# Sixteen scatters into token lists and the zeros behind them, regrouped on one queue of a fused graph-attention and mixture-of-experts kernel

## The chip, the cores and the metric

The kernel runs on one core of a Trainium2 chip. The time is that of the device, in microseconds, from one execution. An engine here is one of the core's instruction streams: PE multiplies matrices, DVE and ACT compute elementwise, POOL and SP in this kernel mostly issue DMAs.

## What is computed

One layer: graph attention over 4096 nodes with 256 features, then a feed-forward layer of eight experts, of which each row uses its two best. Cut to what matters:

```
# attention, 4 heads of 64
h   = einsum('nd,hdk->hnk', layernorm(x), W)
e   = leaky_relu(s_row[:, :, None] + s_col[:, None, :], 0.2)
att = softmax(where(adj > 0, e, -9e15))
y   = elu(att @ h) + layernorm(x) @ Wr + br
x   = x + gamma * normalised(y) + beta
# experts, 8, hidden width 1024, two for each row
xf  = layernorm(x)
top_w, top_i = top_k(xf @ Wg + bg, 2);  top_w = softmax(top_w)
for e in range(8):
    out += w_dense[:, e] * (gelu(xf @ W1[e] + b1[e]) @ W2[e] + b2[e])
x   = x + out
```

## The kernel before, in words

**Two halves.** The first is the attention. The 4096 rows are taken in four passes of 1024, and PE multiplies without a pause while DVE makes the weights. After a pass its rows are finished, normalised and routed (`route_rows`, from L1243): each row gets its two experts, its two weights, and its two places in the *lists*. The lists are a table in HBM, one stretch per expert; a row of it holds the 256 features, both weights, the row's number and its first expert, 260 numbers (1040 bytes). A row is put there by a scatter, an indirect DMA that POOL issues (L1385): 128 rows in one scatter, two for each 128 rows (first and second expert). A pass of 1024 rows makes 16 scatters; 64 in all.

**The expert tiles.** The second half runs over 27 tiles of one expert each (`todo`, L1989): 9 `early` ones of 256 rows, whose rows come from the first two passes, 8 `mid` ones of 256 rows from the first three, then 8 `final` ones of what is left of each expert, and 2 of `rest`. The early and mid tiles are 0 to 16. For a tile, `fetch` (L1777) has SP load the rows of the list (`load_blocks_of`, L579, a small load `known` and eight of `xr`; the first six tiles are loaded whole by L571 instead), then b2 (L1792), W1 (L600) and W2 (L1799). DVE turns the rows (L1857), `up` (L1864) makes 16 matmuls with W1 into PSUM (L1873; 32 records in the trace) and ACT applies GELU to each of the 8 results (L1877), `down` (L1886) makes two products of 128 rows with W2 (L1907), eight matmuls each. DVE weighs each of them into a buffer `o` (L1920; nine buffers, L1919), and POOL adds it to the rows of the result by an indirect DMA with addition, the *sum* (L1932). Two sums of the same rows of the result may not be under way together, so a sum waits until the one before it has landed.

**The last pass inside the tiles.** The 1024 rows of the fourth pass are not finished before the tiles start. Their work is cut into steps and put between the products of the first tiles (`between`, L1975, called twice a tile, after `up` and after `down`). Each half of the pass, 512 rows, ends with eight scatters; the first half after the second call of tile 3, the second after the second call of tile 4. Then the remaining tiles are planned (`plan_rest`, L439).

**The zeros.** Behind the last row of each expert's list, 512 rows of zeros are written (`tail_cleared`, L500, the DMA is L507), so that a tile which reads past the end finds zeros. One is taken off `tails` at the end of each tile.

**What sets the order.** PE's order in the tiles is written out by hand (`order_of`, L543). POOL's order follows from the order in which the program makes the instructions, from dependences, and for the clears from an explicit one: a clear stands behind the last sum made so far (L510 to L514). An early or mid tile's row loads need not wait for scatters or clears made before them (`needs_of`, L557, `declare_no_dep`), for their rows were written long ago. In the other direction nothing is declared: a scatter or a clear waits for the row loads made before it, as both touch the lists. All SP loads and all POOL scatters, sums and clears go through the same queues in this order:

```
2022            between(2 * i + 1)
2023            if tails:
2024                tails.pop(0)()
```

Of the kernel before, what the change touches and what calls it, by code (L numbers as in the profile page):

```python
# [44 lines left out]
def gat_then_moe(  # L45
# [19 lines left out]
    nc = tc.nc  # L65
# [41 lines left out]
    lists = nc.dram_tensor("lists", [E * LIST, RW], F32, kind="Internal").ap()  # L107
# [111 lines left out]
    def forward(apart, stack):  # L219
# [49 lines left out]
        def tables(tag, width):  # L269

            return {
                "expert": moe_tile(f"expert{tag}", [P, width]),
                "mark": moe_tile(f"mark{tag}", [P, width]),
                "own": moe_tile(f"own{tag}", [P, width, E]),
                "place": moe_tile(f"place{tag}", [P, width]),
                "rows": moe_tile(f"rows{tag}", [P, width]),
                "float": moe_tile(f"float{tag}", [P, 2, width]),
                "int": moe_tile(f"int{tag}", [P, 2, width], I32),
                "past": moe_tile(f"past{tag}", [P, width, E]),
                "upto": moe_tile(f"upto{tag}", [P, E]),  # L280
            }
# [61 lines left out]
        early, mid, rest, final, over = tables("e", EARLY), {}, {}, {}, {}  # L343
# [154 lines left out]
        tails = []  # L498

        def tail_cleared(ends, zeros, e):  # L500

            end = nc.values_load(
                ends[0:1, e : e + 1], engines=[mybir.EngineType.Pool],
                min_val=e * LIST, max_val=e * LIST + N,
                skip_runtime_bounds_check_because="a list holds each token at most once",
            )
            clearing.append(nc.gpsimd.dma_start(  # L507
                lists[bass.ds(end, WT), :].rearrange("(p c) d -> p (c d)", p=CH), zeros
            ).ins)
            tc.add_manual_dep(  # L510
                clearing[-1], added[-1].name,
                mybir.DependencyInfo(mybir.DependencyClass.NoSync, mybir.DependencyReason.DATA),
                reason="one list for each tile, behind its sums",
            )  # L514

        clearing, added = [], []

        listed, earlier = [], []

# [21 lines left out]
        ordered, strict = [False], [False]  # L541
# [9 lines left out]
        def entry(t, row, i, top):  # L551
            return nc.values_load(
                t["int"][0:1, row, i : i + 1], engines=[mybir.EngineType.SP],
                min_val=0, max_val=top, skip_runtime_bounds_check_because=why,
            )
# [20 lines left out]
        def rows_of_job(t, i):  # L576
            return FINAL[i] * Q if t is final else TT

        def load_blocks_of(t, i, xb, known, late):  # L579


            first = entry(t, 1, i, E * LIST - WT)
            n = known.shape[1] * CH
            begun = [nc.sync.dma_start(
                known, lists[bass.ds(first, n), D:].rearrange("(c p) d -> p c d", p=CH)
            )]
            rows = lists[bass.ds(first, rows_of_job(t, i)), :]
            for c in range(DC):
                for a in range(P // Q):
                    here = c * P + a * Q  # L590
                    begun.append(nc.sync.dma_start(
                        xb[ts(a, Q), c], rows[:, here : here + Q].rearrange("(k p) d -> p k d", p=Q)
                    ))
            for ins in begun:
                needs_of(ins.ins, late)

        def load_first(t, i, w1):

            e = entry(t, 0, i, E - 1)
            nc.sync.dma_start(w1, W1[bass.ds(e, 1)].rearrange("o (c p) f -> p (o c) f", p=P))  # L600
# [14 lines left out]
        with ExitStack() as layer:  # L615
# [109 lines left out]
            sums = gat.tile([P, DC, NB], F32)  # L725
# [455 lines left out]
            def load_adj(pool, rows, j, n, bufs):  # L1181

                at = pool.tile([P, n, len(rows)], I32, tag="adj", name="adj", bufs=bufs)
                marks["adj"] = nc.sync.dma_start(
                    at,
                    adjT[j * P : (j + n) * P, rows.start : rows.stop].rearrange(
                        "(t p) i -> p t i", p=P
                    ),
                ).ins
                return at  # L1190
# [52 lines left out]
            def route_rows(b, xe):  # L1243
# [100 lines left out]
                at = small.tile([P, 2, n], I32, tag="at", name="at")  # L1344
                nc.vector.tensor_copy(at, pos)
                if b == 0:
# [33 lines left out]
                    yield  # L1380
                    nc.vector.tensor_tensor(others, others, least, OP.max)

                for t in range(n):
                    for k in range(2):
                        ins = nc.gpsimd.indirect_dma_start(  # L1385
                            lists, bass.IndirectOffsetOnAxis(ap=at[:, k, t : t + 1], axis=0),
                            xe[:, t, :], None,
                        ).ins
                        for i in listed:
                            tc.declare_no_dep(ins, i.name, reason="other places of the lists")  # L1390
                        listed.append(ins)

            def finish_blocks(a):

# [80 lines left out]
            def rows_listed():  # L1475
                return fin.tile([P, HB * TB, RW], F32, tag="xe", name="xe", bufs=1)
# [133 lines left out]
            if not apart:  # L1610

                with tc.tile_pool(name="gen", bufs=2) as work:
# [12 lines left out]
                    for b in range(NB):  # L1625
# [4 lines left out]
                        for j in range(NT):  # L1630
                            if j % 2 == 0:
                                at = load_adj(work, mine, j, 2, 2)
# [15 lines left out]
                        for j in range(NT):  # L1648
                            if j % 2 == 0:
                                at = load_adj(work, mine, j, 2, 2)  # L1650
# [126 lines left out]
        def fetch(t, i):  # L1777

            rows = rows_of_job(t, i)
            nch = -(-rows // CH)  # L1780
            chosen = t is early or t is mid
            near = chosen and i + EARLY * (t is mid) < NEAR
            if near:
                xr = full_rows[i]
                known = xr[:, :, D:]
            else:
                xr = work.tile([P, DC, rows // Q, Q], F32, tag="xr", name="xr")
                known = work.tile([CH, nch, RW - D], F32, tag="known", name="known")
                load_blocks_of(t, i, xr, known, chosen)
            e = entry(t, 0, i, E - 1)  # L1790
            b2b = work.tile([CH, D], F32, tag="b2b", name="b2b")
            nc.sync.dma_start(b2b, b2[bass.ds(e, 1)].to_broadcast([CH, D]))  # L1792
            if t is early and i == 0:
                w1 = w10
            else:
                w1 = work.tile([P, DC, F], F32, tag="w1", name="w1")
                load_first(t, i, w1)
            w2 = work.tile([P, FC, D], F32, tag="w2", name="w2")
            nc.sync.dma_start(w2, W2[bass.ds(e, 1)].rearrange("o (c p) d -> p (o c) d", p=P))  # L1799
            job = {"t": t, "i": i, "xr": xr, "known": known, "w1": w1, "w2": w2, "nch": nch, "b2b": b2b}  # L1800
            job["rows"], job["near"] = rows, near
            job["last"] = t is rest and i == SURE - 1

            job["into"] = out[: N - R] if t is early or t is mid else out
            return job
# [163 lines left out]
        xe = rows_listed()  # L1969
# [5 lines left out]
        def between(n):  # L1975
            if n == 0:
                begun.append(turn_sums(ud))
            for half in range(HB):
                if n == 2 * half:
                    begun.append(last_block(  # L1980
                        b0 + half, u[:, half], begun[0][:, :, :, half], given[half],
                        xe[:, ts(half, TB)],
                    ))
                if n >= 2 * half and ordered[0]:
                    if next(begun[1 + half], "end") == "end" and half == HB - 1:
                        ordered[0] = False
                        plan_rest()

        todo = [(early, i) for i in range(EARLY)] + [(mid, i) for i in range(MID)]  # L1989
# [4 lines left out]
        jobs = [fetch(*todo[0])]  # L1994
        given = []

        def load_full(i):
            xr = work.tile([CH, 2, RW], F32, tag="early", name="early", bufs=NEAR - 1)
            load_rows_of(early, i, xr)
            full_rows.append(xr)  # L2000
# [8 lines left out]
        xT = turn(job)  # L2009
        for i in range(len(todo)):  # L2010
            if i + 1 == len(jobs) and i + 1 < len(todo):
                jobs.append(fetch(*todo[i + 1]))
            nxt = jobs[i + 1] if i + 1 < len(todo) else None
            hT = up(job, xT)
            between(2 * i)
            if nxt:
                xT = turn(nxt)
            giving = down(job, hT)
            next(giving)
            if nxt:  # L2020
                next(giving, None)
            between(2 * i + 1)
            if tails:
                tails.pop(0)()
            job = nxt

        def held(k, top):
# [82 lines left out]
```

## Time and profile before

| | us |
|---|---|
| median of three timed runs | 1259.73 (1257.01 to 1262.62) |
| the profiled execution, timed as the others | 1258.36 |
| its span, first to last instruction | 1256.7 |
| first product of the expert tiles (tile 0) | 777 |
| tiles 6 to 16, where rows are loaded by blocks | 871.7 to 1028.4 |
| 16 scatters of the last pass on POOL | 846.5 to 878.8 |
| 8 clears on POOL | 882.6 to 976.9 |

The page gives each engine's busy time first, then the span in 40 slices, one digit a slice (9 is 90% or more), with the clock granted to PE and the busy share of the 16 DMA engines:

```profile
PE   9999999999999999999999999999999999999997
POOL 4000000001002601006110024135222212122222
PEclk9999999999999999999999999999999999999999
DMA  6333533436533646335375423868898897455662
```

A slice is 31.4 us. From slice 24 on (the expert tiles) the DMA engines are at six to nine tenths, before that mostly at three to five. The groups of POOL's DMAs (count, busy time and mean of one in ns, idle time before them and what ended it):

```profile
L1932 POOL DMA_INDIRECT out<-o,ids x66 | 102.3, 1550 | 325.0 <-DMA out<-o,ids 151.0
L1385 POOL DMA_INDIRECT lists<-xe,at x64 | 89.0, 1391 | 268.0 <-issue 184.8
```

An idle time of POOL costs the kernel nothing by itself. `PEld` is the loading of stationary operands, beside the products. The name behind an arrow is what released the instruction after its wait.

### The profile page before, as it was taken

The page shows a single profiled execution, that of the slowest core. Times are in us where ns is not written, and L with a number is a line of the kernel's source. Part 1 is how long each engine was busy: PE and PEld are TensorE (multiplying, and loading weights), DVE is VectorE, ACT ScalarE, POOL GpSimd, SP SyncE. Part 2 cuts the span into 40 slices and gives each one's busy share as a digit, 9 for nine tenths or more (in the row PEclk, how much of TensorE's full clock was granted, in tenths as well). Part 3 has the DMA queues.
Part 4 walks back from the last instruction along what each step waited for, and adds up shares of the span by engine and source line. Part 5 has one row for each costly group of instructions (what it writes and reads, how often), then busy time and mean ns, then how long its engine had stood idle before and what let it go on. Part 6 is the DMA issues. An engine that isn't in the chain of part 4 may idle for free.

```text
span 1256.7 us, 22720 instructions
## 1 busy us (share of the span) xinstructions
PE 1239.8 (99%) x8872; PEld 647.8 (52%) x8872; DVE 845.1 (67%) x1566; ACT 448.2 (36%) x918; POOL 241.3 (19%) x217
## 2 busy tenths in 40 slices
PE   9999999999999999999999999999999999999997
PEld 5444444332232332332325334888888876666686
DVE  7998887879999989999999996845111211111120
ACT  4332322265522375322655232533332332222322
POOL 4000000001002601006110024135222212122222
PEclk9999999999999999999999999999999999999999
DMA  6333533436533646335375423868898897455662
GB/s 215 118 119 110 167 111 102 157 113 139 181 110 107 224 116 201 107 98 157 112 171 191 122 84 103 269 181 230 218 234 213 215 229 144 106 139 106 138 161 36
DMA packets 155541, 190.23 MB, mean 151 GB/s; under 512 B 72312, under 2 KB 125680, under 8 KB 155040
## 3 DMA queue, kind: packets, MB, share of 16 engines
q1 hardware_dynamic: 133392, 145.39, 39.8%
q0 software_dynamic: 20544, 36.74, 13.2%
q10 hardware_dynamic: 1488, 6.55, 1.4%
q8 instruction: 71, 1.16, 0.4%
q14 instruction: 46, 0.38, 0.1%
HBM read 155.77 MB, written 29.74 MB: 148 GB/s over the span
## 4 chain that ended last, share of the span: by engine, by line
PE 93%; DVE 3%; issue 1%; ACT 1%; DMA 1%; another core or an unknown queue 0%; POOLq 0%; SPq 0%; DVEq 0%; ACTq 0%
PE acc L1198 33%; PE po L1907 18%; PE ph L1873 17%; PE den L1207 17%; PE pr L1053 2%; DVE w L1689 2%; PE ph L1101 2%; PE ptx L1253 0%; DMA early<-lists 0%; PE acc L894 0%; PE pt L780 0%; PE ptr L1491 0%; PE po L1946 0%; PE pl L1264 0%; PE po L875 0%
## 5 line engine op out<-in xcount | busy, mean ns | idle before, releaser
L1198 PE MATMUL acc<-w,ha 128*32 128x512 f32 x4096 | 669.9, 593 | 1.3 <-ACT u L1401 0.9
L1689 DVE SCALAR_TENSOR_TENSOR w<-er,eb,am 128x1024 f32<-128x1024 f32 x496 | 606.1, 1275 | 31.1 <-PE den L1207 31.1
L1207 PE MATMUL den<-w,unit 128*2 128x512 f32 x2048 | 466.9, 592 | 0.1
L1198 PEld LDWEIGHTS acc<-w,ha 128*32 128x32 f32 x4096 | 184.5, 110 | 292.8 <-issue 253.9
L1606 ACT ACTIVATE am<-adj 128x1024 bf16<-128x1024 int32 x124 | 130.6, 1054 | 346.5 <-DVE w L1689 211.7
L1873 PE MATMUL ph<-xT,w 128*128 128x256 f32 (+5 forms) x864 | 231.4, 425 | 2.9 <-ACT hT L1877 2.6
L1907 PE MATMUL po<-w,hT 128*128 128x256 f32 (+1 forms) x1040 | 230.2, 380 | 0.0
L1877 ACT ACTIVATE hT<-ph,bias 128x256 f32<-128x256 f32 (+5 forms) x216 | 111.1, 517 | 292.8 <-issue 185.7
L1907 PEld LDWEIGHTS po<-w,hT 128*128 128x128 f32 (+1 forms) x1040 | 196.2, 189 | 31.5 <-issue 3.1
L1873 PEld LDWEIGHTS ph<-xT,w 128*128 128x128 f32 x864 | 163.8, 191 | 63.4 <-issue 38.7
L1920 DVE SCALAR_TENSOR_TENSOR o<-po,share,b2s 128x256 f32<-128x256 f32 (+2 forms) x66 | 31.5, 479 | 230.1 <-PE po L1907 186.4
L1207 PEld LDWEIGHTS den<-w,unit 128*2 128x2 f32 x2048 | 93.5, 85 | 148.2 <-issue 139.8
L1932 POOL DMA_INDIRECT out<-o,ids x66 | 102.3, 1550 | 325.0 <-DMA out<-o,ids 151.0
L1385 POOL DMA_INDIRECT lists<-xe,at x64 | 89.0, 1391 | 268.0 <-issue 184.8
L1857 DVE STREAM_TRANSPOSE xT<-xr 128x512 f32<-128x512 f32 (+5 forms) x21 | 17.9, 851 | 57.1 <-PE ph L1873 31.2
L1053 PE MATMUL pr<-wr,xT 128*128 128x256 f32 x128 | 30.4, 381 | 0.2 <-ACT er L1147 0.2
L1895 ACT ACTIVATE b2s<-b2b,share 128x256 f32<-128x256 f32 x68 | 30.0, 498 | 0.0
L1121 POOL DMA_DIRECT2D residual<-rb x6 | 4.7, 784 | 121.2 <-DVE rb L1068 121.2
L1441 POOL DMA_DIRECT2D xf<-in_x x6 | 8.1, 1351 | 102.2 <-ACT xf L1440 102.2
L1053 PEld LDWEIGHTS pr<-wr,xT 128*128 128x128 f32 x128 | 24.1, 190 | 5.4 <-issue 0.9
L1101 PE MATMUL ph<-wall,xT 128*128 128x264 f32 x96 | 24.6, 399 | 0.0
L207 ACT ACTIVATE m<-y,off 128x256 f32<-128x256 f32 x48 | 23.7, 495 | 1.1 <-DVE off L215 0.6
(394 smaller groups left out, 617.9 us busy)
## 6 DMA issues: line engine op xcount, KB each, us to landing
adj<-in_adj SPq DMA_DIRECT2D x126, 512.0 KB
w<-in_L_ffn_W SPq DMA_DIRECT2D x54, 1024.0 KB
er<-parts ACTq DMA_DIRECT2D x3, 2048.0 KB
lists<-zeros POOLq DMA_DIRECT2D x8, 520.0 KB
residual<-rb POOLq DMA_DIRECT2D x8, 512.0 KB
rb<-residual SPq DMA_DIRECT2D x8, 512.0 KB
out<-y POOLq DMA_DIRECT2D x8, 512.0 KB
xb<-in_x SPq DMA_DIRECT2D x7, 512.0 KB
```

The costliest lines, as they stand in the source:

```text
L1053: order_of(nc.tensor.matmul(pr[:, k, :], turned[b][:, c, ts(t0 + k, P)], wr[:, c, :], start=(c == 0), stop=(c == DC - 1),))
L1101: order_of(nc.tensor.matmul(phs[t - t0], xT[:, c, ts(t, P)], wall[:, c, :], start=(c == 0), stop=(c == DC - 1),))
L1198: queue(nc.tensor.matmul(acc[half][h // 2][here : here + Q, :], ha[:, j, h * K + g * Q : h * K + (g + 1) * Q], w[half][h], start=(j == 0), ...
L1207: queue(nc.tensor.matmul(den[here : here + HB, :], unit[:, j, h, 1 - half : 1 - half + HB], w[half][h], start=(j == 0 and half == 0), stop ...
L1385: ins = nc.gpsimd.indirect_dma_start(lists, bass.IndirectOffsetOnAxis(ap=at[:, k, t : t + 1], axis=0), xe[:, t, :], None,).ins
L1606: nc.scalar.activation(am, at, AF.Relu, scale=2.0)
L1689: marks["w"] = nc.vector.scalar_tensor_tensor(wh[:, these], er[:, these, h], eb[:, j, h : h + 1], mask[:, these], op0=OP.max, op1=OP.min,).ins
L1873: order_of(nc.tensor.matmul(ph, job["w1"][:, c, ts(f, P)], xT[:, c, :], start=(c == 0), stop=(c == DC - 1),))
L1877: job["gelu"] = nc.scalar.activation(hT[:, f, :], ph, AF.Gelu, bias=job["bias"][:, f : f + 1]).ins
L1907: order_of(nc.tensor.matmul(po[:size], hT[:, f, k * CH : k * CH + size], w2[:, f, :], start=(f == 0), stop=(f == FC - 1),))
L1920: given_out.append(nc.vector.scalar_tensor_tensor(o[:size], po[:size], share[:size, k : k + 1], b2s[k][:size], op0=OP.mult, op1=OP.add,).ins)
L1932: added.append(add().ins)
```

## The change

The eight scatters of each half of the last pass are no longer issued where the half ends. They are kept as functions in a list `writes`, and two of them are called after each call of `between`, the first ones after the second call of tile 3, so four a tile. Like the clears they now stand behind the last sum made so far on POOL. The clears start when no scatter is left, and then two are taken a tile, not one. The scatters and clears themselves, their number, sizes and data are the same.

```diff
+            behind_sums(clearing[-1])
+
+        def behind_sums(ins):
+
             tc.add_manual_dep(
-                clearing[-1], added[-1].name,
+                ins, added[-1].name,
                 mybir.DependencyInfo(mybir.DependencyClass.NoSync, mybir.DependencyReason.DATA),
...
+                def write(t, k, behind=False):
+                    ins = nc.gpsimd.indirect_dma_start(
+                        lists, bass.IndirectOffsetOnAxis(ap=at[:, k, t : t + 1], axis=0),
+                        xe[:, t, :], None,
+                    ).ins
+                    for i in listed:
+                        tc.declare_no_dep(ins, i.name, reason="other places of the lists")
+                    listed.append(ins)
+                    if behind:
+                        behind_sums(ins)
+
                 for t in range(n):
                     for k in range(2):
-                        ins = nc.gpsimd.indirect_dma_start(
...
-                        listed.append(ins)
+                        if ordered[0]:
+                            writes.append(partial(write, t, k, True))
+                        else:
+                            write(t, k)
...
+        def write_some():
+            for write in writes[:2]:
+                writes.remove(write)
+                write()
+
...
             if i + 1 == len(jobs) and i + 1 < len(todo):
+                assert todo[i + 1][0] in (early, mid) or not writes + tails
                 jobs.append(fetch(*todo[i + 1]))
...
             between(2 * i)
+            write_some()
...
             between(2 * i + 1)
-            if tails:
-                tails.pop(0)()
+            write_some()
+            for clear in [] if writes else tails[:2]:
+                tails.remove(clear)
+                clear()
```

`ordered` is true only while the last pass is worked into the tiles, so the 48 scatters of the first three passes go out as before. The order of POOL's DMAs in the tiles, before and after:

```
before: sums 3, 8 scatters, sums 4, 8 scatters, clear, sums 5, clear, sums 6, ... clear, sums 12, sums 13 ...
after:  sums 3, 4 scatters, sums 4, 4 scatters, sums 5, 4 scatters, sums 6, 4 scatters, sums 7, 2 clears,
        sums 8, 2 clears, sums 9, 2 clears, sums 10, 2 clears, sums 11 ...
```

More of the change, by code (lines that the diff above doesn't have):

```diff
@@ L509, in tail_cleared @@
             ).ins)
+            behind_sums(clearing[-1])
+        def behind_sums(ins):
             tc.add_manual_dep(
-                clearing[-1], added[-1].name,
+                ins, added[-1].name,
                 mybir.DependencyInfo(mybir.DependencyClass.NoSync, mybir.DependencyReason.DATA),
-                reason="one list for each tile, behind its sums",
+                reason="a part for each tile, behind its sums",
             )
-        clearing, added = [], []
+        clearing, added, writes = [], [], []
         listed, earlier = [], []
@@ L1381, in route_rows @@
                     nc.vector.tensor_tensor(others, others, least, OP.max)
+                def write(t, k, behind=False):
[8 more added lines that the diff above has]
+                        behind_sums(ins)
                 for t in range(n):
                     for k in range(2):
[L1385 to L1390, printed above, removed]
-                        listed.append(ins)
+                        if ordered[0]:
+                            writes.append(partial(write, t, k, True))
+                        else:
+                            write(t, k)
             def finish_blocks(a):
```

## The prediction, made before the changed kernel had run

> **What bounds the kernel now.** I read the page's busy times and the chain of waits first, then the stretches of single expert tiles, then the one place where their rhythm breaks, and last the queues that the change touches (POOL and SP).
>
> ```profile
> PE 1239.8 (99%) x8872; PEld 647.8 (52%) x8872; DVE 845.1 (67%) x1566; ACT 448.2 (36%) x918; POOL 241.3 (19%) x217
> PE 93%; DVE 3%; issue 1%; ACT 1%; DMA 1%; another core or an unknown queue 0%; POOLq 0%; SPq 0%; DVEq 0%; ACTq 0%
> ```
>
> TensorE is busy 99% of the span and makes 93% of the chain. POOL, the only engine whose order changes, is not among the chain's shares. So the moved instructions can gain only what they cost TensorE elsewhere. All idle time of PE is 1256.7 - 1239.8 = 16.9 us, and I look for it in the expert tiles. The stretch view, cut where tiles 5, 6, 7 and 8 begin (columns: length, busy time of PE, PEld, DVE, ACT and POOL, granted clock, DMA share, GB/s):
>
> ```profile
> 858.00:871.74 13.74, 13.74 (x65) 12.09 (x66) 12.87 (x92) 4.58 (x10) 5.39 (x5) 1.00 0.76 214
> 871.74:890.29 18.55, 15.78 (x65) 13.04 (x64) 2.35 (x9) 4.36 (x10) 8.06 (x9) 0.91 0.89 256
> 890.29:904.10 13.81, 13.81 (x65) 12.16 (x64) 2.43 (x9) 4.58 (x10) 4.05 (x4) 1.00 0.81 186
> ```
>
> A tile costs 13.81 us with PE never idle. Tile 6 has the same instructions and costs 18.55: 4.74 us more, of which 18.55 - 15.78 = 2.77 are idle PE and 15.78 - 13.81 = 1.97 slower products. It is the only tile that does so. The chain of waits in it:
>
> ```profile
> 871.90 4.95 PE ph L1873 x20
> 876.85 0.02 issue
> 876.87 0.47 ACT hT L1877
> 877.34 3.09 another core or an unknown queue
> 880.43 0.02 issue
> 880.98 2.08 PE ph L1873 x4
> ```
>
> The GELU that should follow 0.4 us after its product waits 1.87 us (the timeline of ACT), the next one 3.11. Its releaser has no name in the trace, although the records of the products it needs start before 876.1. So the profile shows that the release came late, not why. What ran beside it, from POOL's timeline:
>
> ```profile
> 868.92 1.00 POOL L1385 DMA_INDIRECT lists<-xe,at  x1 [0.30 <-DVE intf L417]
> ...
> 877.87 0.97 POOL L1385 DMA_INDIRECT lists<-xe,at  x1 [0.30 <-issue]
> 882.63 0.58 POOL L507 DMA_DIRECT2D lists<-zeros  x1 [3.79 <-DMA lists<-xe,at]
> 883.52 1.60 POOL L1932 DMA_INDIRECT out<-o,ids  x1 [0.30 <-issue]
> 889.99 1.57 POOL L1932 DMA_INDIRECT out<-o,ids  x1 [4.87 <-DMA out<-o,ids]
> ```
>
> These are the last eight scatters in a row, 868.92 to 878.84. The first eight stand at 846.50 to 856.41. The stretch view of both bursts:
>
> ```profile
> 846.00:857.00 11.00, 11.00 (x55) 9.71 (x54) 3.38 (x20) 4.39 (x11) 7.97 (x9) 1.00 0.79 176
> 868.90:878.90 10.00, 9.31 (x42) 7.52 (x41) 3.63 (x22) 1.89 (x4) 7.78 (x8) 1.00 0.93 293
> ```
>
> The first burst costs PE nothing, at a DMA share of 0.79. The second meets a load of w2 (SP, 871.93) and the eight row loads of a tile (874.63 to 881.74), at 0.93 and 293 GB/s, and there the break lies.
>
> **What the Trainium skill says.** "DMA: Bandwidth & Descriptors", section "Issuing engines are not separate DMA queues": DMAs of POOL and SP run on the same 16 engines and interleave. The two bursts above agree: share and GB/s rise when SP's loads join. "Perfetto Trace Analysis", section "DMA Instruction — SWDGE (GPSIMD)": the recorded time of a POOL DMA is that of writing descriptors, not of moving data. The trace agrees: the clear at 882.63 still waits for scatters whose last record ended at 878.84. "TensorE: Matmul & The Clock Gate", section "What's actually happening": PE's clock is halved for a window of about 3.4 us after an idle one. Tile 6 agrees in size: 0.09 of 18.55 us missing clock is 1.67 us, which is half of 3.3.
>
> **The change part by part.**
>
> *Order.* PE, DVE, ACT and SP keep their instructions in the same order; only POOL's changes. Before: sums of tile 3, 8 scatters, sums of tile 4, 8 scatters, then a clear ahead of the two sums of each of the tiles 5 to 12. After: 4 scatters each behind the sums of tiles 3, 4, 5 and 6, then two clears each behind the sums of tiles 7, 8, 9 and 10. The counts stay: 16 scatters at 0.97 us are 15.6 us of POOL either way, 8 clears 7.2 us. Direct gain: 0, as POOL is busy 8.06 of 18.55 us even in tile 6.
>
> *Bursts of eight go.* Four scatters take 4 x 1.27 = 5.1 us of POOL (0.97 and 0.30 between). By POOL's order they fall after the sum at 867.04, so 868.9 to 874, and the next four behind both sums of tile 5. The second burst then ends before the row loads of 874.63 begin, and the pile of scatters, w2 and row loads is not built at that place. If this pile held up the releases, all 4.74 us go: idle time and the halved clock that follows it. Bounds: nothing is gained (cause elsewhere), or 4.74. A gain above that has no source that I see: the other gaps of PE in the tiles are under 0.6 us each and at transposes of tiles 1 to 5. I take 4.74.
>
> *Sums.* Those of tile 5 wait behind eight scatters and the clear's 3.79 us: DVE made them by 870.73 and 872.48, POOL issues them at 883.52 and 889.99. With four scatters ahead, the first can go at about 874.4. In tiles 7 to 10 a second clear (1.05 us and its data) stands ahead of the sums. A late sum costs PE something only when the nine o buffers are all held; at two sums in 13.81 us they cover 62 us, against a largest lag of 889.99 - 872.48 = 17.5. Cost: 0; without that cover DVE's o would stop and PE with it.
>
> *Added waits.* The third scatter of a group waits for the row loads issued ahead of it on SP, since both touch the lists. Behind it on POOL are only the other scatter and the sums, covered as above. Before, each clear had this wait and went at once behind its sum (891.11 behind 889.99). Cost: 0 to 2 us of POOL, none of PE.
>
> *Two clears a tile.* This is the part with a price. A clear writes 520 KB, as much as four scatters. How far SP's loads lag shows in DVE's wait for the rows of a tile:
>
> ```profile
> 901.77 0.71 DVE L1857 STREAM_TRANSPOSE xT<-xr 128x512 f32<-128x512 f32 x1 [0.38 <-DMA xr<-lists]
> 931.15 0.71 DVE L1857 STREAM_TRANSPOSE xT<-xr 128x512 f32<-128x512 f32 x1 [2.13 <-DMA xr<-lists]
> 960.45 0.71 DVE L1857 STREAM_TRANSPOSE xT<-xr 128x512 f32<-128x512 f32 x1 [3.81 <-DMA xr<-lists]
> 989.61 0.71 DVE L1857 STREAM_TRANSPOSE xT<-xr 128x512 f32<-128x512 f32 x1 [5.34 <-DMA xr<-lists]
> ```
>
> It grows by (5.34 - 0.38) / 6 = 0.83 us a tile while one clear a tile goes out, and is 4.0 at 1002.1, after the last. So a clear costs SP's chain about 0.8 us. The next o stands behind this wait on DVE and frees the PSUM buffer that PE takes again one tile later: the one after 989.61 starts at 990.25, its product ended at 987.0, PE needs the buffer at 997.3. That leaves 6.6 us of cover at the worst place. With two clears the lag grows by 1.7 a tile over four tiles, 6.6 in all: the same total as before, earlier. Upper bound by bytes: 520 KB at 220 GB/s are 2.4 us a clear, 8 x 2.4 = 19. I take 0.83, thus no cost to PE, and keep the other for the range.
>
> *Sum.* Span 1256.7 - 4.74 = 1252.0. Around it lie 1258.36 - 1256.7 = 1.7 us, so 1253.6 against that execution's 1258.36. The three timed runs have a median of 1259.73, 1.4 above it, and none lies below 1257.01, 3.4 above 1253.6: each had a loss of this size somewhere. Against their median the forecast is -0.49%.
>
> **Rivals.** *The break stays or moves* (1258.5). For it: the release has no name, the first burst did no harm, and four scatters and later two clears still meet row loads; after 1003 the DMA share is about 1.0. Against it: in those very tiles, at shares of 0.8 to 1.0 with a clear or sums in each, no tile but this one breaks. One break of the same size at another place gives 1258.4; half of one 1256.
>
> *The break goes, but the zeros take PE's cover* (1268). Place: tiles 8 to 13. Price: up to 2.4 us a clear, 19 us of lag; cover from no wait at all is 6.6 + 5.3 = 11.9; PE waits 7.3, in about four pieces, one a tile, each with up to 1.7 us of halved clock behind it: 1253.6 + 7.3 + 6.8 = 1267.7. It decides from 11.9 / 8 = 1.5 us a clear on; to make the kernel slower than before at all it must reach some 2. Against it: 0.83 in the trace, and the scatters around tiles 4 and 5, twice these bytes a tile, where SP still waits 3 to 4.5 us for PE to free w2.
>
> *The scatters don't spread*: excluded by POOL's order of the changed kernel.
>
> **How the numbers follow.** Break gone 0.66, stays or moves 0.19, zeros take the cover 0.15. The likeliest gives 1253.6, by itself 1251.5 to 1256. Half a per cent, about what a measurement of this kernel can tell from no change, is 6.3 us: the line is at 1253.4, in the middle of that case. As the timed runs of before lie above the profiled one on the whole, I count somewhat more than two thirds of the case (0.48) below the line. Of the second case 0.02 is faster (timed runs that break more often than the profile), 0.15 the same, 0.02 slower; of the third 0.13 slower, 0.02 the same. So faster 0.48 + 0.02 = 0.50, same 0.18 + 0.15 + 0.02 = 0.35, slower 0.15. The range takes the first case whole and the second to its upper side: 1250.5 to 1261.
>
> **What would show it.** Right: tile 6 takes 13.8 us at full clock, no GELU waits for an unnamed releaser, POOL has four scatters between pairs of sums, DVE's wait for rows peaks near 6 us around tile 11. Wrong: another tile of 16 us or more; PE waiting for DVE's o or for w in tiles 8 to 13; a clear that costs DVE's wait 1.5 us or more.

## The result, and the profile after

| us, median (lowest to highest, runs) | before | after |
|---|---|---|
| timed runs of one set | 1258.74 (1254.81 to 1262.62, 13) | 1254.04 (1253.56 to 1255.56, 13) |
| profiled execution | 1258.36 | 1254.18 |
| its span | 1256.7 | 1252.5 |

The ratio after to before on record is 0.9971, with a 95% interval of 0.9959 to 0.9982: 0.29% faster, less than the half per cent that the prediction took as its line, and clear of no change within this set. (It is not the quotient of the two medians, which is 0.9963.) More telling than the median is the spread: 7.8 us before, 2.0 after, and even the lowest of before is above the median of after.

The page's busy times and the chain of waits of the changed kernel:

```profile
PE 1237.9 (99%) x8872; PEld 647.5 (52%) x8872; DVE 845.1 (67%) x1566; ACT 448.2 (36%) x918; POOL 241.8 (19%) x217
PE 94%; DVE 3%; issue 1%; ACT 1%; DMA 0%; POOLq 0%; SPq 0%; DVEq 0%; ACTq 0%
```

PE does the same 8872 products in 1.9 us less, which is the halved clock that is gone. The stretch view cut at the beginnings of tiles 5, 6, 7 and 8, with the same columns as before:

```profile
858.08:872.06 13.98, 13.98 (x68) 12.33 (x66) 12.51 (x91) 4.58 (x10) 6.41 (x6) 1.00 0.79 176
872.06:885.87 13.81, 13.81 (x65) 12.16 (x65) 2.43 (x9) 4.58 (x10) 6.17 (x6) 1.00 0.89 213
885.87:899.68 13.81, 13.81 (x65) 12.16 (x65) 2.43 (x9) 4.47 (x10) 6.27 (x7) 1.00 0.91 229
```

Tile 6 takes 13.81 us with PE never idle and the clock full. At the beginning of tile 7 the changed kernel is 890.29 - 885.87 = 4.42 us ahead; at the end of the span 4.2. Almost nothing was given back after the place where it was won. Note the DMA share of tile 6: 0.89 in both kernels (at 256 GB/s before, 213 now). The same busy share of the DMA engines now does no harm. POOL's timeline around it:

```profile
881.16 0.99 POOL L1388 DMA_INDIRECT lists<-xe,at  x1 [0.30 <-DMA xr<-lists]
...
885.03 0.97 POOL L1388 DMA_INDIRECT lists<-xe,at  x1 [0.30 <-issue]
886.30 1.60 POOL L1944 DMA_INDIRECT out<-o,ids  x1 [0.30 <-issue]
893.92 1.56 POOL L1944 DMA_INDIRECT out<-o,ids  x1 [6.02 <-issue]
895.79 1.00 POOL L1388 DMA_INDIRECT lists<-xe,at  x1 [0.31 <-DMA xr<-lists]
```

Four scatters lie between pairs of sums, as POOL's order said. Releases are not all on time even so: just behind the third four, the second GELU of a tile waits 1.02 us where the usual is 0.34, and two are then done together.

```profile
886.82 0.47 ACT L1889 ACTIVATE hT<-ph,bias 128x256 f32<-128x256 f32 x1 [6.55 <-issue]
888.32 0.84 ACT L1889 ACTIVATE hT<-ph,bias 128x256 f32<-128x256 f32 x2 [1.02 <-PE ph L1885]
```

PE has no idle time from it. The timeline of DVE, for its wait for a tile's rows:

```profile
898.19 0.71 DVE L1869 STREAM_TRANSPOSE xT<-xr 128x512 f32<-128x512 f32 x1 [1.38 <-DMA xr<-lists]
912.97 0.71 DVE L1869 STREAM_TRANSPOSE xT<-xr 128x512 f32<-128x512 f32 x1 [2.35 <-DMA xr<-lists]
...
930.43 0.71 DVE L1869 STREAM_TRANSPOSE xT<-xr 128x512 f32<-128x512 f32 x1 [5.99 <-DMA b2b<-in_L_ffn_b]
...
945.47 0.71 DVE L1869 STREAM_TRANSPOSE xT<-xr 128x512 f32<-128x512 f32 x1 [7.22 <-DMA b2b<-in_L_ffn_b]
...
959.37 0.71 DVE L1869 STREAM_TRANSPOSE xT<-xr 128x512 f32<-128x512 f32 x1 [7.30 <-DMA xr<-lists]
...
996.87 0.71 DVE L1869 STREAM_TRANSPOSE xT<-xr 128x512 f32<-128x512 f32 x1 [3.37 <-DMA xr<-lists]
```

DVE waits up to 7.30 us, and less again once the last pair of clears is out (952.95). (Two of the waits are put down to `b2b`, which SP loads just behind the rows.) Most of the rise is one step, from 2.35 to 5.99 us. PE never waits for it.

So the break is gone. Open are three things: what made it, why its size varied by 8 us over the timed runs of one program, and what the pairs of clears cost.

### The profile page after: what moved, and what is told of

It reads as the page before. It is cut to its first block, busy times and chain, and to the rows that moved or that the text cites. A ratio compares the mean times of both kernels' runs of the same rounds, so it can differ in the third digit from the quotient of the medians.

```text
span 1252.5 us, 22714 instructions
## 1 busy us (share of the span) xinstructions
PE 1237.9 (99%) x8872; PEld 647.5 (52%) x8872; DVE 845.1 (67%) x1566; ACT 448.2 (36%) x918; POOL 241.8 (19%) x217
## 3 DMA queue, kind: packets, MB, share of 16 engines
q10 hardware_dynamic: 1488, 6.55, 1.5%
## 4 chain that ended last, share of the span: by engine, by line
PE 94%; DVE 3%; issue 1%; ACT 1%; DMA 0%; POOLq 0%; SPq 0%; DVEq 0%; ACTq 0%
PE acc L1202 33%; PE po L1919 18%; PE ph L1885 17%; PE den L1211 17%; PE pr L1057 2%; DVE w L1701 2%; PE ph L1105 2%; PE ptx L1257 0%; DMA early<-lists 0%; PE acc L898 0%; PE pt L784 0%; PE ptr L1503 0%; PE po L1958 0%; PE pl L1268 0%; PE acc L748 0%
```

## The experiments

A *release* is the event that lets a waiting instruction start; a *break* is a stretch of idle PE in the tiles. Four sets of runs were made, each on one chip, with the kernel before timed among them. In the expectations, "the pile" (later theory 1 or A) is that scatters in a row, together with the loads beside them, hold up releases; "chance" (later 2 or B) is that breaks come in any order of POOL; "burst" (in one run) is that eight in a row do it alone, whatever SP loads; and "zeros" (later 3) puts the difference down to the clears: to the wait of the first one, or to their being taken one or two a tile.

### First set: parts of the change alone

The kernel before had 1258.76 here (67 runs).

*The kernel before again*, without an edit, for a second profile.

> The kernel before, unchanged, profiled once more and timed. Pile theory (a burst of eight scatters that runs into loads of SP holds up PE's releases): the break is again in tile 6, beside the second burst of eight scatters, its length varying between executions, and no other tile of the tiles 5 to 16 takes over 14 us; times between 1254.8 and 1262.6 us. Chance theory (a break that falls anywhere): the long tile is another one or there is none. Zeros theory (the first clear's wait is at fault): the break lies after the eighth scatter, not beside it.

1259.17 (1254.70 to 1265.35, 12 runs). The profile shows two breaks. ACT's timeline, with the idle time ahead of each instruction and its releaser in brackets:

```profile
863.32 1.20 ACT L1877 ACTIVATE hT<-ph,bias 128x256 f32<-128x256 f32 x3 [8.82 <-PE ph L1873]
...
880.35 1.21 ACT L1877 ACTIVATE hT<-ph,bias 128x256 f32<-128x256 f32 x3 [10.61 <-issue]
```

In an undisturbed tile, ACT is idle for 6.55 us between two tiles' GELUs and then does eight one by one. Here it is idle 2 and 4 us longer, and then three are released at once. PE's timeline has the two gaps:

```profile
863.85 4.58 PE L1873 MATMUL ph<-xT,w 128*128 128x256 f32 x20 [1.58 <-ACT hT L1877]
...
880.88 4.58 PE L1873 MATMUL ph<-xT,w 128*128 128x256 f32 x20 [2.95 <-ACT hT L1877]
```

The pile's expectation, a break in tile 6 only, was missed: the first of the two is in tile 5, behind the *first* burst (850.10 to 860.03), which had cost nothing in the profile that the prediction was made from. SP's row loads of that stretch were all issued by 851.4, and their small packets (under 512 bytes) ended at about 853, eight microseconds before the late GELU of tile 5 was due (861); what was in flight later beside the scatters was a load of w1, from 855.82 on. So row loads need not be in flight while the releases are late. They did overlap the first two scatters of the burst.

*The scatters spread, one clear a tile instead of two:*

```diff
-            for clear in [] if writes else tails[:2]:
+            for clear in [] if writes else tails[:1]:
```

> As the changed kernel, but one clear a tile, from tile 7 to tile 14, not two. Pile theory: the spread of the scatters is the whole gain, so 1254.0 us plus or minus 0.3, no break, and DVE's wait for rows grows half as fast. Zeros theory (the gain comes from clearing two at a time): 1258 to 1260 as before.

1255.57 (1253.73 to 1264.56, 22 runs), ratio to before 0.9986 (0.9971 to 1.0002). Its profile has a span of 1252.0 and no break. But the interval just takes in no change, and five of its 22 runs lie above 1260: the median falls between the two expectations, and neither was met. The changed kernel never went above 1260 in 37 runs of three sets; it wasn't in this set, so whether the pair of clears or the set makes the difference stays open.

*The bursts kept, two clears a tile:*

```diff
-            if tails:
-                tails.pop(0)()
+            for clear in tails[:2]:
+                tails.remove(clear)
+                clear()
```

> As the kernel before, both bursts of eight scatters, but two clears a tile, from tile 4 to tile 7. Pile theory: the break in tile 6 stays, 1257 to 1261 us in the median with a spread of several us. Zeros theory: 1254, narrow.

1258.30 (1254.35 to 1261.63, 22 runs), ratio 0.9998 (0.9988 to 1.0009): as before. The chain of waits has the known break at the second burst (870.75 to 880.70 here):

```profile
873.92 3.25 PE ph L1873 x12
877.17 0.02 issue
877.19 0.47 ACT hT L1877
877.67 3.10 another core or an unknown queue
...
881.27 0.97 another core or an unknown queue
```

The clears by themselves neither help nor harm. That leaves the scatters for what the change brings; the copy with the scatters alone, above, points the same way without being clear of noise.

*The bursts kept, but the row loads of tile 8 wait until the scatters have landed:*

```diff
             for ins in begun:
-                needs_of(ins.ins, late)
+                if t is early and i == EARLY - 1:
+                    for other in listed:
+                        after(ins.ins, other, "behind the scatters")
...
+                else:
+                    needs_of(ins.ins, late)
```

> As the kernel before, with both bursts of eight, but the row loads of tile 8, which in the kernel before start in the middle of the second burst, wait until its scatters have landed; the load of w2 still meets the burst. Pile theory: with the row loads out of it the break is gone or below 1 us, 1254 to 1255.5 us; the SP chain comes about 8 us later there, within its 10 us of cover. Burst theory (eight scatters in a row do it alone, whatever SP loads): 1257 to 1261 as before. If the later loads cost PE something, that shows as a wait of up or of turned rows in tiles 8 to 10, and not beside the burst.

1256.83 (1254.88 to 1264.10, 22 runs), ratio 0.9988 (0.9977 to 0.9999). In SP's timeline the edit shows as 10 us of silence behind the load of w2:

```profile
873.15 0.38 SPq L1807 DMA_DIRECT2D w<-in_L_ffn_W  x1
883.21 0.37 SPq L584 DMA_DIRECT2D known<-lists  x1
883.79 4.51 SPq L591 DMA_DIRECT2D xr<-lists  x8
```

and tile 6 ran undisturbed (13.81 us, PE never idle) in this profile, although all eight scatters went in a row from 871.08 to 881.03. It is a gain of 0.1%, at the edge of what the interval shows, and the median lies between the two expectations (1254 to 1255.5, 1257 to 1261). The first burst was left as it was, with row loads issued beside it until 851.2, and no slow run of this kernel was profiled. So whether row loads are a needed part of the pile stays open: this run doesn't say whether what is left of the loss came from the first burst or from the second.

### Second set: more and fewer scatters in a row

*The changed kernel again; the first eight in a row and the second eight spread; four spread and twelve in a row; all sixteen in a row.* The edits of the last three, each alone:

```diff
-                        if ordered[0]:
+                        if ordered[0] and b > b0:
...
-                        if ordered[0]:
+                        if ordered[0] and b == b0:
...
-            for write in writes[:2]:
+            for write in writes[:] if not ordered[0] else []:
```

> The changed kernel once more, unaltered, beside three mixtures of it on one chip, because the copy with one clear a tile was less even than it (up to 1264.6 us). Theory 1 (the pile: eight scatters in a row, landing beside a load of w2 and the rows of a tile, hold up PE's releases): median 1253.5 to 1255.5 us, nine runs in ten below 1257, no idle PE after 836 us in the profile. Theory 2 (chance: the breaks come in any order of POOL, and the changed kernel was lucky in thirteen runs): median 1256 to 1259 and runs spread over 8 us, as the kernel before. Theory 3 (the pair of clears matters, since it moves the loads behind it): even runs here, within 2 to 3 us, where one clear a tile had a tail of five runs in 22 above 1260.

> The first eight scatters go in a row as before, the second eight out two behind each product, and two clears a tile as in the changed kernel. Theory 1 (the pile of the second burst): the burst at 869 to 879 us is gone, so most runs lie at 1254 to 1256 us, with a break of 1.5 to 3 us at 862 us in some of them, as one of three profiles of the kernel before had it; median 1254.5 to 1256.5. Theory 2 (chance): 1256 to 1259. Theory 3 (clears): as even as the changed kernel.

> The mirror of it: of the first eight scatters four go out two behind each product, and the other twelve in a row behind the second product that follows; two clears a tile. Theory 1 (the pile): twelve in a row are 15 us of POOL and half as much again as the second burst, so the break is in nearly every run: an idle PE of 2 to 5 us at 870 to 890 us, median 1257 to 1261. Theory 2 (chance): 1256 to 1259, and no place for the break. Theory 3 (clears): as even as the changed kernel, 1253.5 to 1255.5.

> All sixteen scatters in a row, 21 us of POOL, at the place where the second burst stood, then two clears a tile. Theory 1 (the pile): the break at its longest, 3 to 8 us of idle PE in a profile, and the sums behind it 10 us later than in the kernel before; median 1259 to 1265 us. Theory 2 (chance): 1256 to 1259, as every kernel. Theory 3 (clears): 1253.5 to 1255.5.

| us, median (range, runs) | | ratio to before |
|---|---|---|
| before | 1254.02 (1253.06 to 1257.72, 43) | |
| changed kernel | 1254.19 (1253.71 to 1258.69, 14) | 1.0003 (0.9995 to 1.0011) |
| second eight spread | 1255.02 (1253.35 to 1258.24, 13) | 1.0005 (0.9997 to 1.0013) |
| twelve in a row | 1254.11 (1253.46 to 1256.44, 13) | 1.0002 (0.9994 to 1.0010) |
| sixteen in a row | 1254.41 (1253.71 to 1256.37, 13) | 0.9998 (0.9990 to 1.0006) |

I had not expected this: in this set the kernel before itself takes 1254.02, and no arrangement of the scatters matters. The pile's expectations for twelve and sixteen in a row missed, by 2.9 and 4.6 us. None of the theories had a place for a kernel before that is as fast as the changed one. (It has no profile in this set; the four kernels that have one show no break.) What differed between the sets could be seen in work that no version changes: the share of the 16 DMA engines that the packets of SP's loads took in the first 600 us (columns: queue, packets, MB, share). The first profile of before, and below it the changed kernel in this set:

```profile
q1 hardware_dynamic: 22656, 61.35, 32.9%
```

```profile
q1 hardware_dynamic: 22656, 61.35, 31.8%
```

All profiles of the earlier sets had 32.8 to 33.2%, the four of this set 31.8 to 32.0%. The same packets took 3% longer where the breaks were.

### Third set: the same on another chip

*Before, after and sixteen in a row, unaltered.*

> The kernel before, unaltered, with a profile. In the two sets of runs so far with 1258.7 us for it, the weights' packets of the first 600 us, which no version changes, took 32.8 to 33.2% of the 16 engines; in the set with 1254.0 us they took 31.8 to 31.9%. Theory A (the pile breaks PE's run only where the memory answers more slowly): the two go together: share near 31.8% means 1253.5 to 1255 us and no idle PE at 862 to 890 us, share near 33% means 1257 to 1260 us and 1.5 to 5 us of idle PE there. Theory B (the break is chance of an execution, and the sets differ for another reason): a break, or none, whatever the share.

> The changed kernel, unaltered. Theory A: 1253.5 to 1255.5 us whatever the share of the weights' packets, since no pile is left; ratio to before 0.996 to 0.998 at a share near 33%, 0.9995 to 1.001 at 31.8%. Theory B: it varies as the kernel before does, ratio within 0.999 to 1.001 in both.

> All sixteen scatters in a row, as run in the last set with 1254.4 us. Theory A: at a share near 33% the longest pile breaks PE's run the most, 1258 to 1265 us and 3 to 8 us of idle PE; at 31.8%, 1254 to 1255 us again. Theory B: about as before.

| us, median (range, runs) | | ratio to before |
|---|---|---|
| before | 1257.76 (1255.12 to 1262.37, 23) | |
| before once more, with a profile | 1257.23 (1254.28 to 1260.84, 14) | 0.9994 (0.9982 to 1.0007) |
| changed kernel | 1254.73 (1253.72 to 1257.86, 10) | 0.9978 (0.9965 to 0.9992) |
| sixteen in a row | 1268.83 (1267.12 to 1269.65, 6) | 1.0088 (1.0074 to 1.0103) |

The same program with sixteen in a row takes 1254.41 in one set and 1268.83 in another, and now the order of the scatters matters in the direction that the pile says: sixteen in a row are worse than eight, eight than four. The size for sixteen was missed: 1258 to 1265 us had been expected, with 3 to 8 us of idle PE. The kernel before has one break in its profile here, 1.76 us at the second burst. The share of the loads' packets was 32.6 to 32.9% in this set's three profiles. The profile of sixteen in a row is the best look at the cause, because here it is large. Its stretch view first, in the third set and then in the second (columns as above; scatters in a row from 862.57 to 882.72, and from 863.03 to 883.30):

```profile
866.00:874.00 8.00, 8.00 (x38) 7.04 (x38) 2.75 (x27) 0.22 (x1) 5.97 (x7) 1.00 0.76 228
874.00:882.00 8.00, 0.41 (x2) 0.01 (x1) 2.25 (x10) 0.00 (x0) 6.07 (x7) 0.69 0.37 136
882.00:886.00 4.00, 0.00 (x0) 0.00 (x0) 0.40 (x2) 0.36 (x1) 1.30 (x2) 0.50 0.18 67
```

```profile
866.00:874.00 8.00, 8.00 (x39) 7.04 (x38) 6.19 (x45) 1.11 (x4) 6.17 (x7) 1.00 0.74 213
874.00:882.00 8.00, 8.00 (x38) 7.04 (x38) 0.00 (x0) 3.92 (x9) 6.17 (x7) 1.00 1.05 322
882.00:886.00 4.00, 4.00 (x20) 3.51 (x20) 1.24 (x3) 0.00 (x0) 1.00 (x2) 1.00 0.81 198
```

POOL goes on alike in both: seven scatters in 8 us. PE, ACT and SP's loads stop in the one and not in the other. And they stop while the DMA engines have *little* to do: a share of 0.37 and 0.18, against 1.05 and 0.81 where nothing stops. So this break is not a lack of DMA bandwidth. Nor did the engines wait for their instructions to be brought: the two queues that the page calls `instruction` moved no packet between 866 and 890, and the engines went on at 885.6. What they wait for shows on DVE, which at that time works through a chain of small operations on its own results. Its timeline, third set:

```profile
868.32 0.22 DVE L407 TENSOR_REDUCE rowsf<-pastf 128x8 f32<-128x64 f32 x1 [0.82 <-DVE placef L412]
...
869.72 0.15 DVE L458 TENSOR_SCALAR counts<-rowsf 128x1 f32<-128x1 f32 x1 [1.03 <-DVE newf L482]
...
876.16 0.15 DVE L467 TENSOR_REDUCE counts<-more 128x1 f32<-128x2 f32 x1 [1.18 <-DVE theirsf L479]
...
880.44 0.24 DVE L487 TENSOR_TENSOR sparef<-sparef,theirsf 128x16 f32<-128x16 f32 x1 [1.92 <-DVE theirsf L486]
885.60 0.48 DVE L1932 SCALAR_TENSOR_TENSOR o<-po,share,b2s 128x256 f32<-128x256 f32 x1 [3.90 <-remote]
```

The same operations in the second set:

```profile
867.90 0.22 DVE L407 TENSOR_REDUCE rowsf<-pastf 128x8 f32<-128x64 f32 x1
...
868.18 0.15 DVE L458 TENSOR_SCALAR counts<-rowsf 128x1 f32<-128x1 f32 x1
...
869.16 0.14 DVE L467 TENSOR_REDUCE counts<-more 128x1 f32<-128x2 f32 x1
...
869.80 0.17 DVE L487 TENSOR_TENSOR sparef<-sparef,theirsf 128x16 f32<-128x16 f32 x1
```

This is the clearest reading of the study. In the third set DVE waits 0.8 to 1.9 us for *its own* preceding instruction, which is done and needs no DMA; in the second the operations follow each other without a gap. Data or a busy engine can't be what is missing there; what the trace leaves is the event that tells of an instruction's end, up to 2 us late while scatters pile up. That the event is late is read from these gaps; no record shows the event itself on its way. The profile of before in the first set (`before_again_1`) has the same waits, 0.46 to 1.20 us, beside its second burst. The three other profiles with a break have no such chain of DVE operations beside it, so they can't show the waits. A short one, 0.51 and 0.78 us, is also in two of the changed kernel's three profiles, with no idle PE. The break ends with the pile: the first clear, which waits for the scatters to have landed, starts at 885.42, the o at 885.60, three GELUs at 885.64. ACT's line for these:

```profile
885.64 1.21 ACT L1889 ACTIVATE hT<-ph,bias 128x256 f32<-128x256 f32 x3 [19.41 <-issue]
```

PE starts again behind the first of them:

```profile
886.17 6.82 PE L1885 MATMUL ph<-xT,w 128*128 128x256 f32 x20 [11.75 <-ACT hT L1889]
```

The sum agrees with the clock: PE idle 11.75 us ahead of 886.17, then half speed until 890.73, which costs 4.56 / 2 = 2.28 us; together 14.0, the difference of the two spans (1266.1 and 1252.1).

### Fourth set: two in a row

```diff
-            for write in writes[:2]:
+            for write in writes[:1]:
```

> The changed kernel with one scatter behind each product instead of two, so that two go in a row for a tile and the zeros begin four tiles later. If the harm grows with the scatters in a row (sixteen: 1268.8 us, eight: 1257.8, four: 1254.7, each on a chip whose weights' packets took 32.6 to 32.9%), two in a row are no worse than four: 1253.5 to 1254.8 us, with no own wait of DVE over 0.3 us at 860 to 900 us, where the changed kernel still shows one of 0.5 to 0.8. If four in a row are harmless already, the rest of the changed kernel's spread comes from elsewhere: the same 1254 to 1255 us with the same spread. If the later zeros meet the rows of the last equal tiles: 1256 to 1260 us with PE waits near 1010 us. At a share near 31.8% before itself is at 1254 us and the run tells only the last of these.

1254.50 (1253.59 to 1258.37, 22 runs), before 1256.81 (1254.22 to 1265.79, 27), ratio 0.9978 (0.9966 to 0.9990): no better than the changed kernel in the third set. In its profile DVE has no own wait over 0.3 us, and the zeros, now as late as 1004.42, meet the rows of the last equal tiles without a wait of PE. Twelve of its 22 runs still lie above 1254.3; a part of that may have a reason far from the scatters, told in the last section. This profile has a share of 31.8% for the loads' packets although the times of before were high in this set. So that share, which fitted three sets, does not tell by itself when a break comes.

## Why the prediction was right

*The break and its price: right.* Tile 6 fell from 18.55 to 13.81, all of the 4.74 us. The forecast for the time was 1253.6; the median is 1254.04, the profiled execution 1254.18. The medians differ by 4.70 us. That this is so near to 4.74 is in part luck: the loss of before varies from run to run (1254.81 to 1262.62 us here), and the one execution that was read happened to lie near the median. "Each had a loss of this size somewhere", said of three runs, doesn't hold for the thirteen: the lowest is 1.2 us above the forecast. The medians give -0.37% rather than the forecast's -0.49%, since before over 13 runs has 1258.74 while the three runs known then said 1259.73; 0.4 us (0.03%) are the error of the forecast itself. The recorded ratio, -0.29%, differs from that of the medians by another 0.08%. The chance for "faster" was set with the line in the middle of the likeliest case, and the result fell on the other side of it.

*What makes the break: half right.* Scatters in a row hold up releases; that is shown by sixteen, eight and four in a row in one set. The rest of the prediction's pile did not hold as it stood. Row loads need not be there while releases are late (the break at the first burst); whether they are needed at its beginning is open. The high DMA share of 0.93, which the prediction gave as the sign of the pile, is not a condition: with sixteen in a row the engines stand still at 0.18 to 0.37. And "the first burst did no harm" was read from one execution; in the next profile it cost 1.58 us. The part that the prediction left open, that a release came late and the trace doesn't say why, is now one step further: releases are late for PE, ACT and DVE alike, DVE's for itself included. What slows them was not shown.

*The place of the scatters: right in order, off in time.* The second four were forecast for 868.9 to 874, clear of the row loads; they ran from 862.92 to 867.88, beside the row loads of another tile (859.55 to 867.13), and no break came of it. In that profile, then, distance from row loads is not what kept PE going.

*Sums and added waits: right, at no cost.* The largest lag of a sum fell from 17.5 to 9.2 us. Sixteen in a row put the sums 30 us late in the second set and cost nothing there either, so at least 30 of the 62 us of cover that the prediction gave to the nine o buffers are there. A wait of scatters for SP's row loads, expected of the third of a group, shows at the first of the third and of the fourth group (the lines with DMA xr<-lists), without an idle time beyond the usual 0.3.

*Two clears a tile: right that PE has cover, wrong in the size of the lag.* Predicted was a peak near 6 us; it is 7.30. From 2.35, just behind the first pair, to 7.30 behind the fourth are 4.95 us for six to eight clears, 0.6 to 0.8 each on average. But 0.83 is no constant of a clear, as the prediction took it: 3.64 us come in one step, from 912.97 to 930.43, and then 1.23 and 0.08. If that step is put down to the two clears in it, they cost 1.8 each, above the 1.5 that the prediction named as a sign of being wrong. The two repetitions have such a step too (none to 3.31, and 1.81 to 5.63) and little behind it (peaks 4.55 and 7.08). What stops the rise was not shown. The start was also off: the prediction began at 0.4 and gave the scatters no price, while the wait here is 2.35 by the first pair (0.45, 1.38, 2.35 at 883.80, 898.19 and 912.97); in the repetition of the second set there is none yet at 896.42. With the bursts kept it never exceeds 1.7, perhaps because the break delays PE and so gives the rows time. The total never came near the 19 us that the bytes' bound of 2.4 us a clear would give, on which the losing rival stood.

*The rivals.* "The break stays or moves" fell: no profile of the changed kernel has a break in the tiles 5 to 16, in three sets. Five of its 37 runs are above 1256.5, though, and none of these was profiled. In the second set, by the times of before, there was hardly a break to remove, and the change then brings nothing: 1.0003. "The zeros take PE's cover" is refuted by bursts with two clears a tile and by the changed kernel itself.

*What stays open:* what makes one set, or one execution, prone to the break and another not; by what path scatters delay a release; whether loads must be beside them at its beginning (with sixteen in a row no packet of SP's loads moved from 876 to 885, and the engines stood still all the same); and whether two clears a tile are better than one.

## What to carry to other kernels

A row of scatters on POOL can stop engines that share no data with it, as far as the traces tell by making releases late. So put a few scatters behind each piece of work, where buffers allow the delay; groups of four were short enough here, and groups of two brought no more. To find such a cause, look for an engine that waits for its own last instruction, and make the suspected thing larger, not only smaller: sixteen in a row showed in one profile what eight had only hinted at. And time the kernel before in every set: the same pair of kernels differed by 0.3% in one set and by nothing in the next.

## What the runs showed of the hardware that was not expected

- One program, sixteen scatters in a row, took 1254.4 us on one chip and 1268.8 on another, each within 3 us over its runs. Before, on one chip, had 1258.8 in one set and 1254.0 in a later one.
- Beside scatters in a row, DVE waited 0.5 to 1.9 us for the end of its own preceding instruction. With sixteen in a row ACT waited 19.4 us, 12.9 of them after the product that it needed should have released it (a first GELU follows its tile's first product by 1.1 us in the changed kernel), for the most part with the DMA engines at a share of 0.2 to 0.4.
- The clock's window falls where it falls. "TensorE: Matmul & The Clock Gate" of the Trainium skill, section "What's actually happening", says that the window which decides on it, about 3.4 us, runs freely. The clock records agree with that: behind gaps of 0.32 and 2.45 us in the tiles PE's clock was halved for 3.4 us in one execution of before, and behind a gap of 2.95 us in another not at all. (The prediction took from the same section that a halved window follows an idle one; the length fits, but these gaps were shorter than a window.) And five of the fourteen profiles have 3.4 us of half clock at 8 us from the start, or at 258, which the others, with gaps of under 1 us there like theirs, don't have. Each such window costs up to 1.7 us (half of 3.4). In the second set the two profiles with one have spans of 1253.1 and 1253.3, the two without 1252.0 and 1252.1.
